# Attention and feed-forward over one core: another order of band and feed-forward work, another choice of PSUM banks, stores issued by ScalarE

## The chip, the core and the metric

One core of a Trainium2 chip runs the whole program, in float32. The metric is the device time of one execution in microseconds. Before the change it is 2633.58 us, the median of three runs (2631.95 to 2634.81).

## What is computed

The input x has the shape (2, 256, 128, 128): batch, time T, band FB, channel C. Three residual blocks follow each other:

```python
xt = _ln(x, ln_t_w, ln_t_b).transpose(0, 2, 1, 3)
x = x + _mha(xt, t_wi, t_bi, t_wo, t_bo, 4, causal_mask).transpose(0, 2, 1, 3)   # over time
xf = _ln(x, ln_f_w, ln_f_b)
x = x + _mha(xf, f_wi, f_bi, f_wo, f_bo, 4, band_mask)     # over bands, |i - j| <= 16
xn = _ln(x, ln_n_w, ln_n_b)
h = gelu(xn @ w1.T + b1)                                   # 128 -> 512
x = x + (h @ w2.T + b2)
```

Each attention has 4 heads of 32 channels.

## The kernel before

The work is cut into 384 groups of 512 tokens (NT = 4 tiles of 128). The first 128 groups (`OverTime`) do attention over time and write to DRAM. Then 16 runs follow, each of 8 groups of attention over bands (`OverBands`) and then 8 feed-forward groups (`FeedForward`) on the same tokens. I call them the first to eighth band group and feed-forward group of a run.

`BoundedPath.run` is one loop over n, a software pipeline written out by hand: step n does the scores or the first hidden products of group n, the weighing of group n - 1, the output of group n - 2, and prepares later groups. Every engine keeps the order in which the instructions are written (`InOrder`), so that order alone decides who runs when, and a waiting instruction holds all behind it on its engine.

A group passes through these stages:

- `load` fetches its tokens with a DMA on SyncE, 14 steps ahead; `statistics` (VectorE) and `root` (GpSimd) make mean and inverse deviation.
- `normalize` makes xh in 4 VectorE instructions; `turn` transposes it in blocks of 32 by 32 into z (VectorE) and writes z to the DRAM tile `turned` in 4 DMAs on SyncE; `fetch` reads `turned` back as xnT, channels on partitions. Step n normalizes and turns group n + 3 and fetches group n + 2.
- Band group: `queries_keys` and `values` multiply xnT by wf on TensorE; `take_query`, `take_key`, `take_values` copy the results from PSUM as qT, kT, v on ScalarE. `first_half` makes the scores, `first_function` limits and masks the fourth head on VectorE and applies exp on ScalarE; `first_mask` masks the other three on GpSimd (tile pf). `weigh` multiplies pf by ones (sums, bank rp) and by v (bank op); `invert` takes ln and exp of the sums on ScalarE, `divide` refines that and scales op to oT on VectorE; `output` multiplies oT by wn, `finish` adds the result to the tokens on VectorE. For the eighth band group of a run `invert_exactly` takes the reciprocal on VectorE, since ScalarE then holds the gelu tables.
- Feed-forward group: `first_half` and `second_half` make two hidden products each (xnT by w1f), `gelus` on ScalarE write hT, `weigh` multiplies hT by w2T into one bank zp (16 products), `divide` adds it to res on VectorE, and `store` writes two groups' results at once with 4 DMAs on SyncE.

A product is 4 matmuls side by side, of 32 weight columns each (`product`); in float32 the profile shows each as two matmul records with a weight load each. PSUM has 8 banks of 512 floats. In band and feed-forward steps `bank` hands them out in turn (`turn_of_bank`), with a few held back (`path.held`, `follow`); in the time steps the banks are named.

In a step of the runs TensorE gets, in this order:

```python
do(n, "first_half", "first_function", "first_mask")
do_at(n + 3, (OverBands, FeedForward), "normalize", "turn")
do(n - 1, "weigh")
do(n - 1, "invert_exactly" if turn else "invert")
do(n - 2, "output", "finish")          # band steps
do(n - 1, "divide")
do(n, "second_half", "second_function")
do_at(n + 1, OverBands, "queries_keys", "take_query", "take_key")
do_at(n + 1, OverBands, "values", "take_values")
```

Of the kernel before, what the change touches and what calls it, by code (L numbers as in the profile page):

```python
# [19 lines left out]
P = 128  # L20
H = 4
# [4 lines left out]
NT = 4  # L26
# [343 lines left out]
class Group:  # L370
# [7 lines left out]
    def __init__(self, path, src, dst, before=None, store=None):  # L378
        self.path, self.src, self.dst = path, src, dst
        self.before, self.store = before, store  # L380

# [76 lines left out]
    def turn(self):  # L458
# [3 lines left out]
        z = path.work.tile([P, H, P], F32, name="z", bufs=2)  # L462
# [98 lines left out]
class Attention(Group):  # L561
    which = None
    swapped = ()
# [7 lines left out]
    def queries_keys(self):  # L571
        path = self.path
        wf = path.k.wf[self.which]
        self.qp = path.bank([P, NT * P], "qp", self.place.get("qp", path.held.pop("qp", None)))
        product(path, self.qp, wf[:, 0:P], self.xnT)

        self.kp = path.bank([P, NT * P], "kp", self.place.get("kp"))
        product(path, self.kp, wf[:, P : 2 * P], self.xnT)

    def take_query(self):  # L580
        path = self.path
        self.qT = path.work.tile([P, NT * P], F32, name="qT")
        path.scalar.activation(self.qT, self.qp, AF.Identity, bias=path.k.bq[self.which], scale=1.0)

    def take_key(self):
        path = self.path
        self.kT = path.work.tile([P, NT * P], F32, name="kT")
        path.scalar.copy(self.kT, self.kp)

    def values(self):  # L590
        path = self.path
        wv = path.k.wf[self.which][:, 2 * P : 3 * P]
        self.vp = path.bank([P, NT, P], "vp", self.place.get("vp"))
# [3 lines left out]
    def take_values(self):  # L597
        path = self.path
        self.v = path.work.tile([P, NT, P], F32, name="v", bufs=4)
        path.scalar.copy(self.v, self.vp)  # L600

# [13 lines left out]
    def divide(self):  # L615

        path, vector = self.path, self.path.vector
        if self.r0 is None:
# [3 lines left out]
            vector.tensor_scalar(self.oT, u, -1.0, None, ALU.mult)  # L622
            return
# [4 lines left out]
        vector.tensor_tensor(by_rows(self.oT), by_tile(self.op), by_tile(u), ALU.mult)  # L628

    def output(self):  # L630
        path = self.path
        self.yp = path.bank([P, NT, P], "yp", self.place.get("yp", path.held.pop("yp", None)))
# [3 lines left out]
    def finish(self):  # L636
        self.path.vector.tensor_tensor(self.dst(), self.yp, self.dst(), ALU.add)
        if self.store is not None:
# [14 lines left out]
class OverTime(Attention):  # L653
# [7 lines left out]
    def values(self):  # L661
        path = self.path
        wv = path.k.wf[self.which][:, 2 * P : 3 * P]
        self.vp = [path.bank([P, 2, P], "vp", self.place.get(f"vp{s}")) for s in range(2)]
# [5 lines left out]
    def take_values(self):  # L670
        path = self.path
        self.v = path.work.tile([P, NT, P], F32, name="v", bufs=4)
        for s in range(2):
            path.scalar.copy(self.v[:, 2 * s : 2 * s + 2], self.vp[s])

    def first_tiles(self):
# [3 lines left out]
        self.s0 = {h: path.bank([P, 2, 2 * P], "sp", path.banks[f"a{h}"]) for h in range(H)}  # L680

    def second_tiles(self):
# [3 lines left out]
        self.s1 = {h: path.bank([P, 2, P], "sp", path.banks[f"b{h}"]) for h in range(H)}  # L686
# [15 lines left out]
    def first_weights(self, heads):  # L702
        for h in heads:
            self.path.scalar.activation(self.p0[:, :, h], self.s0[h], AF.Exp)

    def second_weights(self, heads):
        for h in heads:
            self.path.scalar.activation(self.p1[:, :, h, 0], self.s1[h], AF.Exp)

# [803 lines left out]
```

## Time and profile before

| what | value |
|---|---|
| median of three runs | 2633.58 us |
| profiled execution: span on the page (it gives no other time of it) | 2631.9 us |
| TensorE matmuls busy | 2617.8 us, 99% |
| VectorE, GpSimd, ScalarE busy | 2140.8, 1958.6, 1838.8 us |
| DMA, mean over the span | 131 GB/s |
| chain that ended last | 99% TensorE matmuls |
| granted TensorE clock | 1.000 |

The time groups take the first 934 us of the span, the 16 runs the rest. The end of a matmul is modelled in such a profile, and matmuls overlap, so the busy share of TensorE says little on short delays; the starts of its blocks say more. In the timeline a row gives start, length, engine, operation, tiles written and read, shape and count; in square brackets stands how long the engine was idle before and who ended that. In rows of stretches come the length, then busy time and number of instructions of each engine, the clock, the share of the DMA engines and their rate. In rows of waits come the sum, the number and the longest. DMA rows of the page give the size and the time from issue to landing.

### The profile page before, as it was taken

The numbers are of one execution on the slowest core, as the hardware profiler recorded it, in microseconds if no ns is written. First come the engines' busy times: TensorE is split into PE (matmuls) and PEld (weight loads), VectorE is DVE, ScalarE is ACT, GpSimd is POOL, SyncE is SP. The second block draws the span as 40 slices with busy tenths as digits, with TensorE's granted clock in tenths as the row PEclk, the third lists the DMA queues.
The fourth block names the chain that finished last, engine by engine and source line by source line (L and its number), as shares of the span: only waits on it lengthen the run. The fifth ranks groups of instructions, "written<-read, shape, count | busy, mean of one in ns | idle before, by whom it ended". The sixth has DMA issues, their size and how long they took to land.

```text
span 2631.9 us, 156460 instructions
## 1 busy us (share of the span) xinstructions
PE 2617.8 (99%) x68688; PEld 1837.4 (70%) x68688; DVE 2140.8 (81%) x6410; ACT 1838.8 (70%) x3543; POOL 1958.6 (74%) x2311
## 2 busy tenths in 40 slices
PE   9999999999999999999999999999999999999999
PEld 6666666666766767666777776667676677777776
DVE  8888888888888887977878779788797797887974
ACT  7989988999899875564655746647557466475573
POOL 7999999999999987666667666665776666757762
PEclk9999999999999999999999999999999999999999
DMA  6656555565565454445454544554454445554543
GB/s 155 167 149 158 149 149 149 155 155 149 149 158 149 122 127 119 115 123 127 118 124 124 123 122 117 126 128 120 122 126 120 120 119 131 123 120 123 123 104 88
DMA packets 469797, 344.97 MB, mean 131 GB/s; under 512 B 43120, under 2 KB 404464, under 8 KB 469104
## 3 DMA queue, kind: packets, MB, share of 16 engines
q1 hardware_dynamic: 468408, 334.41, 50.5%
q8 instruction: 540, 8.85, 1.5%
q14 instruction: 153, 1.25, 0.2%
q10 hardware_dynamic: 696, 0.46, 0.1%
HBM read 167.98 MB, written 166.72 MB: 127 GB/s over the span
## 4 chain that ended last, share of the span: by engine, by line
PE 99%; DVE 0%; issue 0%; DMA 0%; ACT 0%; ACTq 0%; DVEq 0%
PE bank L907 99%; DMA x<-in_x 0%; DVE xh L907 0%; DVE bank L907 0%; DVE res L907 0%; DVE stats L907 0%; DVE oT L907 0%; DVE u L907 0%; DVE xnT L907 0%; ACTq L907 0%; ACT p L907 0%; DVE vy L907 0%; ACT lnv L907 0%; DVE mv L907 0%; ACT root L907 0%
## 5 line engine op out<-in xcount | busy, mean ns | idle before, releaser
L907 ACT ACTIVATE hT<-bank,b 128x512 f32<-128x512 f32 x512 | 348.1, 688 | 524.2 <-PE bank L907 483.2
L907 POOL TENSOR_SCALAR_AFFINE_SELECT pf<-pf 128x512 f32<-128x512 f32 x768 | 477.7, 637 | 185.3 <-ACT pf L907 159.1
L907 PEld LDWEIGHTS bank<-w2T_sb,hT 128*32 128x32 f32 x16384 | 467.4, 110 | 54.8 <-issue 29.0
L907 PE MATMUL bank<-xnT,wf 128*32 128x512 f32 x4096 | 492.4, 592 | 0.5 <-DVE xnT L907 0.5
L907 PE MATMUL bank<-xnT,w1f 128*32 128x512 f32 x4096 | 486.3, 592 | 0.2 <-issue 0.2
L907 PE MATMUL bank<-w2T_sb,hT 128*32 128x128 f32 x16384 | 482.8, 273 | 1.0 <-issue 1.0
L907 ACT ACTIVATE p<-bank 128x512 f32<-128x512 f32 (+1 forms) x1024 | 430.6, 494 | 62.9 <-PE bank L907 62.9
L907 DVE TENSOR_SCALAR xh<-x,mv,rstd 128x160 f32<-128x160 f32 (+1 forms) x1012 | 394.3, 432 | 59.7 <-POOL rstd L907 49.4
L907 POOL TENSOR_SCALAR_AFFINE_SELECT p<-p 128x1024 f32<-128x1024 f32 (+2 forms) x384 | 364.5, 949 | 57.5 <-ACT p L907 49.1
L907 PEld LDWEIGHTS bank<-wf,xnT 128*32 128x32 f32 x8192 | 243.3, 110 | 144.1 <-issue 101.6
L907 POOL TENSOR_TENSOR p<-p,p 128x512 f32<-128x512 f32 x256 | 324.6, 1291 | 10.6
L907 DVE BATCH_NORM_STATS2 stats<-x 128x6 f32<-128x128 f32 x1536 | 329.0, 276 | 3.4 <-DMA x<-in_x 3.4
L907 POOL TENSOR_SCALAR rstd<-mv 128x4 f32<-128x4 f32 x251 | 57.8, 230 | 361.7 <-DVE mv L907 360.5
L907 PEld LDWEIGHTS bank<-xnT,w1f 128*32 128x32 f32 x4096 | 183.6, 110 | 171.6 <-issue 109.6
L907 PE MATMUL bank<-qT,kT 32*64 32x80 f32 (+4 forms) x16384 | 302.0, 271 | 0.1
L907 PEld LDWEIGHTS bank<-qT,kT 32*64 32x64 f32 x16384 | 260.0, 131 | 51.2 <-ACT kT L907 50.6
L907 DVE TENSOR_TENSOR res<-bank,res 128x512 f32<-128x512 f32 (+1 forms) x259 | 170.3, 658 | 153.3 <-PE bank L907 144.7
L907 ACT ACTIVATE pf<-bank 128x512 f32<-128x512 f32 x512 | 265.8, 602 | 35.5 <-PE bank L907 31.3
L907 PE MATMUL bank<-wn,oT 128*32 128x128 f32 x8192 | 283.8, 274 | 0.1
L907 DVE STREAM_TRANSPOSE z<-xh 128x512 f32<-128x512 f32 x380 | 270.3, 711 | 13.3
L907 PE MATMUL bank<-wf,xnT 128*32 128x128 f32 x8192 | 276.5, 273 | 0.0
L907 POOL TENSOR_TENSOR rstd<-rstd,mhalf 128x4 f32<-128x4 f32 x251 | 260.8, 1039 | 20.9
(100 smaller groups left out, 3820.3 us busy)
## 6 DMA issues: line engine op xcount, KB each, us to landing
turned<-z SPq DMA_DIRECT2D x1520, 64.0 KB, 2.7
xnT<-turned SPq DMA_DIRECT2D x380, 256.0 KB, 3.2
x<-res SPq DMA_DIRECT2D x256, 128.0 KB, 2.5
x<-x SPq DMA_DIRECT2D x128, 256.0 KB, 4.1
out<-res SPq DMA_DIRECT2D x252, 128.0 KB, 2.3
x<-in_x SPq DMA_DIRECT2D x124, 256.0 KB, 4.3
x<-in_x SPq DMA_DIRECT2D x4, 128.0 KB, 2.8
x<-in_x SPq DMA_DIRECT2D x6, 64.0 KB, 2.9
```

The source lines that it names most:

```text
L907: return self.tc.keep_in_program_order(emit(*args, **kwargs))
```

## The change

Five things change, all in the order of work and the choice of banks.

1. In a step whose group and whose next group are both band groups (`bands[2] and bands[3]`), the queries of group n + 1 come before the weighing of group n - 1, and qT is taken right after the inverse of that group; keys and values stay where they were. TensorE's row in a band step, before and then with the change (wf_238 makes queries, keys and values, pf is the weights after exp, the 64x80 rows are scores):

```order
L907 MATMUL bank_112<-pf,ones 32x512 x4
L907 MATMUL bank_113<-pf,v 32x128 x16
L907 MATMUL bank_110<-wn_241,oT 32x128 x16
L907 MATMUL bank_111<-xnT,wf_238 32x512 x4
L907 MATMUL bank_114<-xnT,wf_238 32x512 x4
L907 MATMUL bank_115<-wf_238,xnT 32x128 x16
L907 MATMUL bank_108<-qT,kT 64x80
```

```order
L967 MATMUL bank_108<-qT,kT 64x80
L967 MATMUL bank_109<-xnT,wf_238 32x512 x4
L967 MATMUL bank_114<-pf,ones 32x512 x4
L967 MATMUL bank_113<-pf,v 32x128 x16
L967 MATMUL bank_110<-wn_241,oT 32x128 x16
L967 MATMUL bank_115<-xnT,wf_238 32x512 x4
L967 MATMUL bank_112<-wf_238,xnT 32x128 x16
```

One of the two 512-wide products with wf moved from behind the output to the place between the scores and the sums.

2. In a step between two feed-forward groups (`weigh_around`) the third hidden product stands between the two halves of the weighing of the group before, the fourth behind it. TensorE, one feed-forward step, before and with the change (w1f makes hidden products, w2T weighs them):

```order
L907 MATMUL bank_109<-xnT,w1f 32x512 x4
L907 MATMUL bank_110<-w2T_sb,hT 32x128 x64
L907 MATMUL bank_111<-xnT,w1f 32x512 x4
L907 MATMUL bank_112<-xnT,w1f 32x512 x4
L907 MATMUL bank_113<-xnT,w1f 32x512 x4
L907 MATMUL bank_114<-xnT,w1f 32x512 x4
```

```order
L967 MATMUL bank_114<-xnT,w1f 32x512 x4
L967 MATMUL bank_115<-w2T_sb,hT 32x128 x32
L967 MATMUL bank_112<-xnT,w1f 32x512 x4
L967 MATMUL bank_115<-w2T_sb,hT 32x128 x32
L967 MATMUL bank_110<-xnT,w1f 32x512 x4
L967 MATMUL bank_108<-xnT,w1f 32x512 x4
L967 MATMUL bank_111<-xnT,w1f 32x512 x4
```

The block of 64 matmuls is cut in two, with one hidden product between.

3. `turn_ahead`: from the second run on, the steps of the last three feed-forward groups also normalize and turn the fourth to sixth band group of the next run, and the first two band steps the seventh and eighth. Band steps three to five then have no normalize. VectorE in the step of the sixth feed-forward group, before and with the change (xh and z are normalize and turn, res is the sum after the weighing):

```order
L907 TENSOR_SCALAR xh<-x,mv,rstd 128x5x32 x4
L907 STREAM_TRANSPOSE z<-xh 128x512
L907 TENSOR_TENSOR res<-bank_108,res 128x512
L907 BN_STATS stats<-x 128x6 x4
L907 BN_AGGR mv<-stats 128x2 x4
```

```order
L967 TENSOR_SCALAR xh<-x,mv,rstd 128x5x32 x4
L967 STREAM_TRANSPOSE z<-xh 128x512
L967 TENSOR_SCALAR xh<-x,mv,rstd 128x5x32 x4
L967 STREAM_TRANSPOSE z<-xh 128x512
L967 TENSOR_TENSOR res<-bank_109,res 128x512
L967 BN_STATS stats<-x 128x6 x4
L967 BN_AGGR mv<-stats 128x2 x4
```

A second normalize and turn stands ahead of res; z has three buffers in place of two, `turned` eight in place of three. On SyncE the transposes' DMAs move with them: 8 in these steps, none in band steps three to five.

4. Stores of feed-forward results are issued two steps later (`put`), on ScalarE while the step's group is a feed-forward group, between the second and third gelu; on SyncE otherwise. The last four groups store as before.

5. PSUM banks are taken from a list of free ones, the one that was released first (`take`, `give`), in place of turns.

The core of the diff:

```diff
+    def take(self, name, shape, i=None):
+        free = self.path.free
+        if i is None:
+            i = free[0]
+        if i in free:
+            free.remove(i)
+        self.taken[name] = i
+        return self.path.bank(shape, name, i)
...
+    def weigh_around(self, other):
+        self.zp = self.take("zp", [P, NT, P])
+        self.weigh_tiles(range(0, 2))
+        other.hidden((2,))
+        self.weigh_tiles(range(2, NT))
+        other.hidden((3,))
...
+    def put(self):
+        if not self.prompt:
+            self.store()
...
+        def turn_ahead(n):
+            for i in (n + 3, n + 6):
+                ahead = at(n + 3, OverBands) and at(i, OverBands) and i not in run0
+                if not at(i, OverTime) and (i == n + 3 or ahead) and not at_turn(i):
+                    do(i, "normalize", "turn")
...
+            self.storing = self.scalar if feeds[2] and n < len(groups) - NT else self.sync
+            do_at(n - 2, FeedForward, "put")
...
-            do_at(n + 3, (OverBands, FeedForward), "normalize", "turn")
+            turn_ahead(n)
...
-            do(n - 1, "weigh")
+            if bands[2] and bands[3]:
+                do(n + 1, "queries")
+            if feeds[1] and feeds[2]:
+                groups[n - 1].weigh_around(groups[n])
+            else:
+                do(n - 1, "weigh")
             do(n - 1, "invert_exactly" if turn else "invert")
+            if bands[2] and bands[3]:
+                do(n + 1, "take_query")
...
-            do_at(n + 1, OverBands, "queries_keys", "take_query", "take_key")
+            if bands[2] and bands[3]:
+                do(n + 1, "keys", "take_key")
+            else:
+                do_at(n + 1, OverBands, "queries_keys", "take_query", "take_key")
```

More of the change, by code (lines that the diff above doesn't have):

```diff
@@ L663, in values @@
         wv = path.k.wf[self.which][:, 2 * P : 3 * P]
-        self.vp = [path.bank([P, 2, P], "vp", self.place.get(f"vp{s}")) for s in range(2)]
+        self.vp = [self.take(f"vp{s}", [P, 2, P], self.place.get(f"vp{s}")) for s in range(2)]
         for i in range(NT):
@@ L815, in weigh @@
         path = self.path
-        path.held = {name: path.turn_of_bank() for name in self.follow}
-        self.rp = path.bank([P, NT * P], "rp")
+        self.rp = self.take("rp", [P, NT * P])
         for h in range(H):
@@ L823, in weigh @@
             )
[L824 removed]
+        self.op = self.take("op", [P, NT * P])
         for i in range(NT):
```

110 lines of the change are left out of this document (76 added, 34 removed).

## The prediction

> **What bounds the kernel now.** I read the page first, then the stretches of the 15 full runs (a run is 8 band groups and 8 feed-forward groups), then the timeline of one run, then who waited. The page says TensorE is the bound, and its queue holds one weight load to each matmul. Queue q8 carries 8.85 MB, 64 bytes for each of those 137,376 instructions: it is TensorE's program.
>
> ```profile
> PE 2617.8 (99%) x68688; PEld 1837.4 (70%) x68688; DVE 2140.8 (81%) x6410; ACT 1838.8 (70%) x3543; POOL 1958.6 (74%) x2311
> q8 instruction: 540, 8.85, 1.5%
> ```
>
> A busy PE is not a PE without delays, so I measured what one step costs undisturbed. Feed-forward: from one w2T block to the next.
>
> ```profile
> 1423.95 3.73 PE L907 MATMUL bank<-w2T_sb,hT 128*32 128x128 f32 x126
> 1427.44 0.60 PE L907 MATMUL bank<-xnT,w1f 128*32 128x512 f32 x2
> 1430.88 3.73 PE L907 MATMUL bank<-w2T_sb,hT 128*32 128x128 f32 x126
> ```
>
> That is 6.93 us: 3.49 of w2T and 3.44 of four hidden products, 0.86 each. A band step:
>
> ```profile
> 1376.24 1.90 PE L907 MATMUL bank<-xnT,wf 128*32 128x512 f32 x16
> 1377.96 1.06 PE L907 MATMUL bank<-wf,xnT 128*32 128x128 f32 x32
> 1378.95 0.97 PE L907 MATMUL bank<-qT,kT 32*64 32x80 f32 x64
> 1379.84 1.06 PE L907 MATMUL bank<-pf,ones 128*32 128x512 f32 x8
> 1380.73 1.06 PE L907 MATMUL bank<-pf,v 128*32 128x128 f32 x32
> 1381.60 1.06 PE L907 MATMUL bank<-wn,oT 128*32 128x128 f32 x32
> 1382.47 0.61 PE L907 MATMUL bank<-xnT,wf 128*32 128x512 f32 x4
> ```
>
> That is 6.23 us: queries and keys 1.72, values 0.99, scores 0.89, sums 0.89, p times v 0.87, output 0.87. A run at this pace takes 8 x 6.23 + 8 x 6.93 = 105.3 us. The 15 full runs took (the first, one of the shortest, the sum):
>
> ```profile
> 933.85:1041.82 107.97, 107.97 (x2790) 1.00 0.50 123
> 1362.03:1467.74 105.71, 105.71 (x2758) 1.00 0.48 120
> sum 1593.21, PE 1590.17; mean PE 106.01
> ```
>
> So 1593.2 - 15 x 105.3 = 13.7 us is all that a better order in the runs can win; some 1.5 of it is one-time work in the first run (2,790 matmuls against 2,758). The granted clock is 1.00 throughout. The time phase (until 933.85) keeps its order.
>
> **What the 13.7 us consist of.** First, stops of TensorE with no semaphore behind them:
>
> ```profile
> PE bank L907 <- issue: 2.7, 7, 0.8
> 1143.75:1175.50 31.75, 31.10 (x896) 21.35 (x896) 25.89 (x61) 24.57 (x45) 20.25 (x33) 1.00 0.48 119
> 1568.60:1599.60 31.00, 30.81 (x896) 19.90 (x896) 25.66 (x60) 24.24 (x45) 19.98 (x34) 1.00 0.46 115
> ```
>
> The two stretches run from one such stop to the next; each holds 896 + 896 = 1792 = 7 x 256 instructions, and 256 x 64 bytes is one q8 packet. So TensorE stops where a block of its program ends and the next has not come. The seven idle times make 2.7; each hides about 0.17 more, since an end is modelled 0.27 after its start and the next starts 0.10 after it: 3.9 us. Stops too short for that list I put at 0.7 (estimate): 4.6. Each also shifts the steps behind it; 1.3 for that (estimate).
>
> Second, the end of each run. In the last feed-forward step ScalarE has two gelus, qT and kT in a row, and the scores wait for kT:
>
> ```profile
> 1349.98 0.69 ACT L907 ACTIVATE hT<-bank,b 128x512 f32<-128x512 f32 x1 [3.66 <-PE bank L907]
> 1350.84 0.69 ACT L907 ACTIVATE hT<-bank,b 128x512 f32<-128x512 f32 x1 [0.17 <-PE bank L907]
> 1351.70 0.69 ACT L907 ACTIVATE qT<-bank,bq 128x512 f32<-128x512 f32 x1 [0.17 <-PE bank L907]
> 1352.56 0.59 ACT L907 COPY kT<-bank 128x512 f32<-128x512 f32 x1 [0.17 <-PE bank L907]
> 1352.16 1.22 PE L907 MATMUL bank<-wf,xnT 128*32 128x128 f32 x32
> 1353.31 0.97 PE L907 MATMUL bank<-qT,kT 32*64 32x80 f32 x64
> ...
> 2517.89 1.23 PE L907 MATMUL bank<-wf,xnT 128*32 128x128 f32 x32
> 2519.04 0.97 PE L907 MATMUL bank<-qT,kT 32*64 32x80 f32 x64
> ```
>
> Values to scores is 1.15 here, 0.99 in the steady step: 0.16, in 6 of 15 runs (first and last shown), and half of it in 2 more: 1.1 us.
>
> Third, VectorE in the later band steps. Its limiting of the fourth head, once a step, comes at
>
> ```profile
> 1380.45 0.67 DVE L907 SCALAR_TENSOR_TENSOR bank<-bank,band 128x512 f32<-128x512 f32 x1
> 1386.98 0.67 DVE L907 SCALAR_TENSOR_TENSOR bank<-bank,band 128x512 f32<-128x512 f32 x1
> 1393.53 0.67 DVE L907 SCALAR_TENSOR_TENSOR bank<-bank,band 128x512 f32<-128x512 f32 x1
> 1394.11 1.60 DVE L907 TENSOR_SCALAR xh<-x,mv,rstd 128x160 f32<-128x160 f32 x4
> 1394.23 0.60 ACT L907 ACTIVATE pf<-bank 128x512 f32<-128x512 f32 x1 [0.15 <-DVE bank L907]
> 1395.74 0.71 DVE L907 STREAM_TRANSPOSE z<-xh 128x512 f32<-128x512 f32 x1
> 1396.73 1.13 PE L907 MATMUL bank<-wf,xnT 128*32 128x128 f32 x32
> 1397.79 0.97 PE L907 MATMUL bank<-qT,kT 32*64 32x80 f32 x64
> ```
>
> every 6.54 us where TensorE needs 6.23: VectorE falls 0.31 behind in each step that has a normalize and statistics, until the exp waits for it, then ln, r, qT, kT, and the scores come 1.06 after the values. Such waits, of 0.07 to 0.8, I sum to 2.0 over the runs. The rest, 13.7 - 1.5 - 4.6 - 1.3 - 1.1 - 2.0 = 3.2, is the output of the eighth band group waiting for its exact reciprocal and small waits.
>
> **The change, part by part.** It adds and removes no arithmetic.
>
> Queries ahead of the weighing (TensorE). A product is 8 matmuls and 8 loads. Densest now: scores (128 instructions), sums (16), p times v (64), 48 of the output: 256 in 0.89 + 0.89 + 0.87 + 0.65 = 3.30 us. With the queries behind the scores: 0.89 + 0.86 + 0.89 + 0.87 + 0.44 = 3.95. Feed-forward: 256 of w2T in 3.49; with a hidden product after each half, 1.75 + 0.86 + 1.53 = 4.13. So a block gets some 0.64 us longer to arrive. Of the seven stops, the longest (0.8 + 0.17) would keep 0.35, the others (0.3 to 0.6 with the 0.17) vanish: 3.9 - 0.35, and 0.5 of the short ones: 4.1. From both sides: nothing, if the transfers are late by something else; 4.6 and the shifts behind them, if all go. I take 4.1 and 1.2 of the shifts, since the stops' own length is the nearest row.
>
> qT then comes off the chain into kT: ScalarE takes it once the queries are done, 2.6 us before the keys. In the run's last feed-forward step the third gelu moves ahead of the second w2T half, so only one gelu, qT and kT follow. Counted from the end of the fourth hidden product, the gelu and qT take 2 x 0.86 = 1.72, which is when the keys end; kT then takes 0.17 + 0.59 and is there at 2.5, and the values end at 1.72 + 0.87 = 2.6. The 1.1 goes.
>
> Normalizing early (VectorE). One normalize is 1.60 + 0.71 = 2.3 us. Fourth to sixth group move to the last three feed-forward steps, so band steps three to five lose 2.3 of their 6.5; the feed-forward steps hold two normalizes, one statistics (0.86 + 0.36) and one res (0.69), 6.5 of 6.93: it fits, with nobody near (the first consumer is a step away). The lag of 0.31 starts only in the last steps: 1.7 of 2.0. The rest term gives perhaps 1.4 of 3.2, through less lag before the reciprocal: between 0 and 3.2, taken below the middle since the reciprocal itself stays.
>
> Stores on ScalarE. SyncE takes 3.0 for four; ScalarE's own issues at the start are 0.46 each, so 1.8 to 3.0.
>
> ```profile
> 0.80 0.92 ACTq L907 DMA_DIRECT2D x<-in_x  x2
> 1423.54 1.49 ACT L907 ACTIVATE hT<-bank,b 128x512 f32<-128x512 f32 x2 [0.23 <-PE bank L907]
> 1428.32 3.02 SPq L907 DMA_DIRECT2D out<-res  x4
> ```
>
> Behind them wait the third and fourth gelu. The second ends 1.08 after w2T starts (1425.03); with stores the third ends by 1.08 + 3.0 + 0.69 = 4.8, and the fourth hidden product ends at 5.2. So nothing is late: cost 0, and SyncE is relieved. What they store was finished a step before. Banks by order of release: in the steady step each is written at least one block after its last reader; 0.
>
> Sum: 4.1 + 1.2 + 1.1 + 1.7 + 1.4 = 9.5. Against the profiled execution's 2631.9 (the page gives its span alone, which equals the lowest run, 2631.95) that is 2622.4; the median shown, 2633.6, is 1.7 above it: 2624.
>
> **Rivals.**
> *The stops stay* (the blocks come late whatever the spacing, or other blocks fall badly): 4.1 and 1.2 are lost, 9.5 - 5.3 = 4.2 remain: 2629. For it: seven stops in some 340 blocks are a tail of the transfer times, and the longest exceeds what is won. Against it: both stops above fall exactly on block ends. The Trainium skill's Runtime: NRT & Kernel Launch, Instruction fetch mechanics, says that the fetch of the next page is mostly hidden, because the sequencer issues more slowly than the pages fill; by that rule this rival would hold with no gain at all from spacing. The trace disagrees with "hidden" here, in seven places and 2.7 us of idle.
>
> *The waits only move*: two normalizes make VectorE late for res or the first band steps, which takes the 1.7, 1.4 and some fetch gain again: 9.5 - 3.1 - 2 = 4.4 at best, worse 0: about 2632. Against it: 6.5 of 6.93.
>
> *The inputs come late* (slower). The queries need xnT 0.89 + 0.87 + 0.87 = 2.6 us earlier. SyncE issues the load only when the transposed pieces have landed:
>
> ```profile
> SPq L907 <- DMA turned<-z: 511.2, 445, 4.3
> 1377.71 0.34 SPq L907 DMA_DIRECT2D xnT<-turned  x1
> xnT<-turned SPq DMA_DIRECT2D x380, 256.0 KB, 3.2
> ```
>
> 1377.71 + 3.2 = 1380.9, used at 1382.47 now: 1.6 spare, 2.6 asked, so 1.0 lost in each of 5 band steps of 15 runs: 75 us less 9.5, about 2699. It decides as soon as the load is not issued 1.0 earlier. Against it: groups four to six are turned three steps sooner, and SyncE's list has no transposes in band steps three to five, so the load follows at once. Only the first run keeps the old place.
>
> **How the numbers follow.** Forecast 0.64, stops stay 0.16, waits move 0.12, inputs late 0.08. A change under 0.2% (5.3 us) can't be told from none. Forecast counts as faster; of stops-stay 0.10 as faster (some spacing gain) and 0.06 as the same; waits-move 0.10 the same, 0.02 slower. Faster 0.74, same 0.16, slower 0.10. Range: below, all 13.7 less the one-time 1.5 and a last run's 0.5, 2633.6 - 12.7 = 2621, and 1.5 for the spread of medians: 2619.5; above, the stops-stay case at 2629 and half a microsecond: 2630. That leaves 0.18 out.
>
> **What would show it.** Right: runs of about 105.5 us each; issue waits on TensorE after 933 of under 1 us; values to scores 0.99 in every step; limiting of the fourth head at a pitch of 6.23 in band steps three to five; four out stores on ScalarE between the second and third gelu. Wrong: TensorE idle on the queries' xnT after the scores, or on res or hT; stops at block ends as before; a feed-forward step over 6.93.

## The result, and the profile after

The changed kernel takes 2647.89 us (median of 5 runs, 2644.80 to 2651.86), the kernel before 2633.58 (5 runs, 2631.95 to 2634.81): a ratio of 1.0052, with a 95% interval of 1.0040 to 1.0064. It is slower by half a per cent, where 2624 was forecast. The profiled execution took 2645.76 us (span 2643.8). Its granted clock is 0.999 against 1.000, and undisturbed steps are as long as before (6.23 and 6.93 us), so the clock does not explain the loss.

The page's busy times, and all waits of TensorE for others in the runs (us in all, times, longest):

```profile
PE 2626.4 (99%) x68688; PEld 1872.6 (71%) x68688; DVE 2143.9 (81%) x6410; ACT 1831.9 (69%) x3543; POOL 1960.4 (74%) x2311
```
```profile
PE bank L967 <- DVE ok L967: 4.2, 1, 4.2
PE bank L967 <- ACT pf L967: 1.5, 1, 1.5
PE bank L967 <- issue: 1.1, 1, 1.1
PE bank L967 <- ACT kT L967: 0.2, 1, 0.2
```

The forecast's mark for the stops ("issue" near 1 us instead of 2.7) is nearly met, and a new wait of 4.2 us, for VectorE's `ok`, stands on top. Both together are far from the 11.9 us by which the span grew. The rest shows only in the lengths of the runs: the first, three others and the sum of the 15 full ones.

```profile
933.46:1048.01 114.55, 110.26 (x2791) 76.52 (x2786) 96.82 (x290) 64.22 (x113) 80.58 (x106) 0.99 0.49 121
1048.01:1154.25 106.24, 106.24 (x2757) 76.95 (x2752) 85.44 (x258) 62.95 (x105) 69.97 (x97) 1.00 0.49 123
...
1687.54:1793.59 106.05, 106.05 (x2757) 76.95 (x2752) 85.47 (x258) 63.05 (x105) 69.93 (x97) 1.00 0.50 125
1793.59:1899.63 106.04, 106.04 (x2757) 76.93 (x2753) 85.45 (x258) 62.93 (x105) 69.95 (x97) 1.00 0.48 119
...
sum 1605.45, PE 1598.24 PEld 1156.72 DVE 1293.21 ACT 946.39 POOL 1059.98; mean PE 106.55 PEld 77.11 DVE 86.21 ACT 63.09 POOL 70.67
```

The sum is 12.2 above the 1593.21 of before: 6.6 in the first run (114.55 against 107.97), 5.7 in the other fourteen. And a run in which nothing special happens takes 106.04, where its best before was 105.70: something costs a little in every run, and TensorE counts as busy all the while.

To find it I cut each run into 16 steps, from the start of one weighing on TensorE to the start of the next, and summed each step over the second to the fifteenth run (worked out from the starts; a start that the moved queries shift by their 0.86 is set back; the step that is left out, from the sums of the eighth group to the first w2T, is 4.32 in both):

| step of the run | before, usual length | after | after less before, 14 runs |
|---|---|---|---|
| band steps 1 to 3 | 5.36, then 6.23 | the same, with single longer ones up to 7.95 | +5.1 |
| band steps 4 and 5 | 6.23, with longer ones up to 7.46 | 6.23 | -4.0 |
| band step 6 (VectorE behind) | 6.23 to 6.49 | 6.21 | -1.5 |
| band step 7 (sums of the eighth group at its end) | 6.06 | 6.48 | +5.6 |
| first feed-forward step (exact reciprocal) | 7.88 to 7.95 | 8.02 | +1.5 |
| feed-forward steps 2 to 6 | 6.93 | 6.93 | -0.4 |
| last full feed-forward step | 8.81 or 8.97 | 8.99 | +1.4 |
| first step of the next run | 7.12, up to 7.85 | 7.12, up to 7.49 | -1.9 |

**The first run.** The rows around the verdict, a product of 6 columns computed once (start, us, engine, what, and in brackets the idle time before it and what ended it):

```profile
1016.24 0.39 PE L967 MATMUL bank<-tests,ones 128*128 128x6 f32 x2
1018.20 0.71 DVE L967 STREAM_TRANSPOSE z<-xh 128x512 f32<-128x512 f32 x1
1018.84 0.65 DVE L967 TENSOR_TENSOR res<-bank,res 128x512 f32<-128x512 f32 x1
1020.46 0.32 DVE L967 TENSOR_SCALAR ok<-bank 128x1 f32<-128x1 f32 x4
1020.84 3.43 PE L967 MATMUL bank<-xnT,w1f 128*32 128x512 f32 x16 [4.21 <-DVE ok L967]
```

`verdict` asks for the bank that is first on the list of free ones, but does not take it off. The hidden product behind it gets the same bank, and has to wait until VectorE, which is busy with normalizing, has read the verdict.

**The step of the masks.** GpSimd's masks and TensorE's sums, before and then after:

```profile
1393.70 0.23 POOL L907 TENSOR_SCALAR rstd<-mv 128x4 f32<-128x4 f32 x1 [1.28 <-DVE mv L907]
1395.02 3.94 POOL L907 TENSOR_SCALAR_AFFINE_SELECT pf<-pf 128x512 f32<-128x512 f32 x6
1398.68 1.38 PE L907 MATMUL bank<-pf,ones 128*32 128x512 f32 x8
```
```profile
1801.80 0.69 DVE L967 TENSOR_TENSOR x<-bank,x 128x512 f32<-128x512 f32 x1 [2.78 <-PE bank L967]
...
1824.69 0.23 POOL L967 TENSOR_SCALAR rstd<-mv 128x4 f32<-128x4 f32 x1 [1.27 <-DVE mv L967]
1825.01 1.04 POOL L967 TENSOR_TENSOR rstd<-rstd,mhalf 128x4 f32<-128x4 f32 x1
1826.02 7.91 POOL L967 TENSOR_SCALAR_AFFINE_SELECT pf<-pf 128x512 f32<-128x512 f32 x12
...
1829.20 1.44 PE L967 MATMUL bank<-pf,ones 128*32 128x512 f32 x6
1830.09 0.61 PE L967 MATMUL bank<-pf,v 128*32 128x128 f32 x8
1830.47 0.60 PE L967 MATMUL bank<-pf,ones 128*32 128x512 f32 x2
```

Before, six masks end at 1395.02 + 3.94 = 1398.96, 0.28 after the sums begin; three of the four heads are masked one after the other, so only the last is late, and barely. After, the first six of the twelve end at 1826.02 + 3.95 = 1829.97, 0.77 after the sums' start. Six of the eight sums start at 1829.20, the two of the head masked last only at 1830.47, and in between TensorE runs p times v for other heads. That is why this wait stands in no list: one group of 32 columns waits, the others go on, and TensorE is "busy". The length of the step shows it. Here the Trainium skill's TensorEngine Tiling (Array Packing), Key Properties, fits: tiles operate independently and can load weights and multiply in parallel. The trace agrees, with those two products 1.27 us behind the other six.

**The last feed-forward step.** Values, kT, scores:

```profile
1782.22 0.69 ACT L967 ACTIVATE hT<-bank,b 128x512 f32<-128x512 f32 x1 [1.40 <-PE bank L967]
1783.08 0.69 ACT L967 ACTIVATE qT<-bank,bq 128x512 f32<-128x512 f32 x1 [0.17 <-PE bank L967]
1783.54 1.22 PE L967 MATMUL bank<-wf,xnT 128*32 128x128 f32 x32
1783.94 0.59 ACT L967 COPY kT<-bank 128x512 f32<-128x512 f32 x1 [0.17 <-PE bank L967]
1784.69 0.97 PE L967 MATMUL bank<-qT,kT 32*64 32x80 f32 x64
```

Values to scores is 1.15, now in nearly every run, though ScalarE waits 1.40 us in front of the last gelu: it is not late. kT starts 0.40 after the values start. The experiments say more on where the 0.16 is from.

### The profile page after: what moved, and what is told of

It reads as the page before. It is cut to its first block, busy times and chain, and to the rows that moved or that the text cites. A ratio compares the mean times of both kernels' runs of the same rounds, so it can differ in the third digit from the quotient of the medians.

```text
span 2643.8 us, 156378 instructions
## 1 busy us (share of the span) xinstructions
PE 2626.4 (99%) x68688; PEld 1872.6 (71%) x68688; DVE 2143.9 (81%) x6410; ACT 1831.9 (69%) x3543; POOL 1960.4 (74%) x2311
## 4 chain that ended last, share of the span: by engine, by line
PE 96%; DVE 2%; POOL 1%; DMA 0%; ACT 0%; issue 0%; ACTq 0%; DVEq 0%; POOLq 0%
PE bank L967 96%; POOL pf L967 0%; DVE xh L967 0%; DVE stats L967 0%; POOL rstd L967 0%; DMA xnT<-turned 0%; ACT pf L967 0%; DVE z L967 0%; DVE mv L967 0%; DVE res L967 0%; DVE ln L967 0%; DMA x<-in_x 0%; POOL x L967 0%; DVE x L967 0%; DVE gs L967 0%
## 5 line engine op out<-in xcount | busy, mean ns | idle before, releaser
L967 PEld LDWEIGHTS bank<-w2T_sb,hT 128*32 128x32 f32 x16384 | 517.1, 110 | 87.8 <-issue 26.9
L967 PE MATMUL bank<-xnT,w1f 128*32 128x512 f32 x4096 | 547.6, 594 | 4.2 <-DVE ok L967 4.2
L967 PE MATMUL bank<-w2T_sb,hT 128*32 128x128 f32 x16384 | 534.1, 273 | 0.0
L967 PE MATMUL bank<-xnT,wf 128*32 128x512 f32 x4096 | 514.7, 595 | 1.2 <-DMA xnT<-turned 0.5
L967 PE MATMUL bank<-wn,oT 128*32 128x128 f32 x8192 | 290.5, 274 | 0.3 <-issue 0.2
L967 PEld LDWEIGHTS bank<-xnT,w1f 128*32 128x32 f32 x4096 | 207.2, 110 | 109.6 <-issue 39.1
L967 DVE TENSOR_TENSOR bank<-bank,r 128x512 f32<-128x512 f32 x240 | 166.9, 695 | 102.2 <-PE bank L967 79.1
```

What stands on the lines that cost most here:

```text
L967: return self.tc.keep_in_program_order(emit(*args, **kwargs))
```

## The experiments

On the chips of the experiments the kernel before took 2630.5 to 2632.4 us (medians); ratios are to its runs beside each, with 95% intervals. By its ratio the changed kernel would take about 2645.5 there. The lengths are worked out as above. A step's length is the commonest one, and the full run is that of runs without a longer step (of e6 the median).

| kernel | us | ratio | step 7 | reciprocal | last | full run |
|---|---|---|---|---|---|---|
| changed | 2647.9 | 1.0052 (1.0040 to 1.0064) | 6.48 | 8.02 | 8.99 | 106.04 |
| e1 bank | 2639.5 | 1.0030 (1.0019 to 1.0041) | 6.46 | 8.02 | 9.00 | 106.04 |
| e2 roots | 2643.8 | 1.0044 (1.0031 to 1.0058) | 6.06 | 8.40 | 8.83 | 105.86 |
| e3 stores on SyncE | 2651.9 | 1.0076 (1.0062 to 1.0090) | 6.46 | 8.02 | 9.00 | 106.04 |
| e4 queries back | 2637.7 | 1.0025 (1.0015 to 1.0034) | 6.06 | 7.88 | 8.81 | 105.35 |
| e5 w2T in one piece | 2644.0 | 1.0050 (1.0037 to 1.0064) | 6.46 | 8.02 | 8.99 | 106.03 |
| e6 no early normalizing | 2652.1 | 1.0074 (1.0060 to 1.0087) | 6.06 to 6.70 | 8.02 | 8.99 | 107.3 |
| e7 all orders undone | 2636.3 | 1.0016 (1.0006 to 1.0025) | 6.06 | 7.88 | 8.82 | 105.72 |
| e8 queries in first step | 2631.4 | 0.9996 (0.9987 to 1.0006) | 6.06 | 7.88 | 8.83 | 105.32 |
| e9 stores behind gelus | 2631.5 | 0.9995 (0.9986 to 1.0004) | 6.06 | 7.88 | 8.83 | 105.33 |
| e10 finish behind divide | 2753.0 | 1.0454 (1.0437 to 1.0470) | 6.06 | 7.81 | 8.83 | 112.65 |
| e13 banks alone | 2630.6 | 1.0001 (0.9992 to 1.0010) | 6.06 | 7.95 | 8.97 | 105.70 |
| e14 output ahead | 2648.7 | 1.0069 (1.0056 to 1.0083) | 6.06 | 7.86 | 8.94 | 106.69 |
| e15 stores of before | 2629.8 | 0.9995 (0.9986 to 1.0004) | 6.06 | 7.88 | 8.83 | 105.32 |

### The verdict's bank (e1)

```
-        tp = self.bank([P, 6], "tp", self.free[0])
+        i = self.free.pop(0)
+        tp = self.bank([P, 6], "tp", i)
...
+        self.release(i)
```

> The changed kernel, with the bank of the verdict's product taken off the list of free banks until VectorE has read it. Theory A (a one-time wait for a bank): in the first run the hidden product right behind the verdict waited 4.46 us for VectorE's ok, and three waits of 0.39 us followed; the step was 13.27 us where the kernel before took 7.54. With a bank of its own it goes back to about 7.5 and the step behind it from 7.18 to 6.93: 2647.9 - 6.0 = 2641.9 us, all other steps as in the changed kernel. Rival (VectorE is simply late there, whatever bank): the step stays above 12 us and the time at 2647.9.

The bank is given back behind VectorE's reads. The step went from 13.27 to 7.54 us, that behind it from 7.18 to 6.93, and the time to 2639.5, 6.0 below the 2645.5. Theory A holds: 6 of the 14 us come from a bank that was not taken off the list.

### The root behind the masks (e2)

```
-            if n + 4 in early:
-                do(n + 4, "root")
...
             do(n, "first_half", "first_function", "first_mask")
+            if n + 4 in early:
+                do(n + 4, "root")
```

> The changed kernel, with GpSimd's root of an early feed-forward group put behind the masks of the step instead of in front of them. Theory B (masks late): queries in front of the sums push the output product 0.86 us back, VectorE's finish, divide and statistics hang on it, the root on the statistics, and the masks stand behind the root; the sums of the last band group but one wait for the masks, 0.41 us in every run (6.48 against 6.06 us). Without the root in front, that step is 6.06 to 6.10 in every run: 16 x 0.4 = 6 us, 2641.8 us. Rival C (ScalarE's exps are late since qT stands in front of them): the masks can't start earlier, the step stays at 6.48 and the time at 2647.9. The last band step's output, which waits for the exact reciprocal, may move by 0.1 either way in both.

Step 7 came back to 6.06 as theory B has it, and the exps were early enough: rival C falls. But the time fell by 1.7 only, not 6, and the intervals of the two overlap. The root, now behind the masks, delays the normalize and with it the exact reciprocal behind that on VectorE, and the output of the eighth group waits for its oT, in 14 runs:

```profile
PE bank L967 <- DVE oT L967: 5.2, 14, 0.4
```

The reciprocal's step grew from 8.02 to 8.40. The lateness was handed on, not taken away.

### Who issues the stores (e3)

```
-            self.storing = self.scalar if feeds[2] and n < len(groups) - NT else self.sync
+            self.storing = self.sync
```

> The changed kernel with all stores of the results issued by SyncE again. Theory D (ScalarE's issues are hidden, as predicted): the last feed-forward step stays at 9.85 us in every run; a store on SyncE's list in front of loads can only make an xnT later: 2647 to 2650 us. Rival E (3.0 us of issues between the second and the third gelu hold qT and kT up): that step goes from 9.85 to 9.69 in all 15 runs, 15 x 0.16 = 2.4 us less: 2645.5 us.

The last step stays at 9.00 (9.86 by its shifted start), so rival E falls. The time is some 6 us above the changed kernel's (the intervals just touch), where theory D allowed 2 (2650 against 2647.9). TensorE's waits for xnT are 1.2 us in the profiled execution, and the first steps of the runs are longer by up to 1.1; the rest of the 6 is not explained.

### Queries back behind the output (e4)

```
-            if bands[2] and bands[3]:
+            ahead = False
+            if ahead:
                 do(n + 1, "queries")
...
-            if bands[2] and bands[3]:
+            if ahead:
                 do(n + 1, "keys", "take_key")
             else:
```

> The changed kernel with the queries of the next band group behind the output again, where they stood before; all other parts kept. Theory B says that the queries ahead cost: the step with the late masks back to 6.06 (-6 us), the step with the exact reciprocal from 8.02 to 7.89 (-2), the xnT late in the second and third band steps gone (-5 in the profiled execution), against some 2 us of stops at the ends of program blocks in the band steps that come back: 2647.9 - 11 = 2637 us. Rival F (the feed-forward order or the two normalizes are what costs): the band steps give nothing and the stops come back: 2648 to 2651 us.

2637.7, as theory B said; rival F falls. All three steps come back at once: 6.06, 7.88 and, in all 15 runs, 8.81. An undisturbed run is 105.35 where the floor of steps is 105.3.

### Feed-forward order, early normalizing (e5, e6)

e5 calls `weigh` and then `second_half` in place of `weigh_around`; e6 has

```
-            for i in (n + 3, n + 6):
+            for i in (n + 3,):
```

> The changed kernel with the second feed-forward product in one piece again (hidden products three and four behind it, as before). On this chip the changed kernel would take about 1.0052 x 2631.8 = 2645.5 us. Theory H (the interleaved feed-forward order does what was predicted, but there is little to do): the stops at block ends in the middle feed-forward steps come back, 1.2 us over the runs of the kernel before and 0.1 with the interleaved order; the last feed-forward step keeps its 0.16, since that comes from columns of TensorE that run apart after the sums waited for masks: 2646 to 2648 us. Rival F (the interleaved order is what costs): the last feed-forward step loses its 0.16 in 15 runs and the one-time wait of 6 us in the first run goes: 2637 us.

> The changed kernel without the early normalizing: groups are normalized and turned three steps ahead, as before; queries still ahead. Theory of the prediction's slower rival (inputs late): the load of xnT stands on SyncE behind transposed pieces that hang on VectorE's normalize of the same step, up to 1.0 us late in each of 5 band steps of 15 runs, 75 us at most: between 2660 and 2720 us, with TensorE idle in front of the queries. Rival (two normalizes in a step cost more than early inputs bring): 2645.5 or less, no idle in front of the queries.

e5 is the same as the changed kernel within the intervals: the interleaved order neither costs nor brings anything that can be measured. Neither theory H's 1 to 2 us nor rival F's gain shows.

e6 is 6 us slower than the changed kernel, and between the two expectations (2660 and more, 2645.5 or less). The waits are there, but they are small:

```profile
PE bank L967 <- DMA xnT<-turned: 16.2, 16, 2.1
PE bank L967 <- DVE ok L967: 2.0, 1, 2.0
```

That is 16.2 us, in 16 of the 75 steps that the expectation counted, where it had up to 75 us. And the wait for the verdict is half as long, since VectorE has one normalize in that step instead of two: half of the 4.2 comes from the early normalizing.

### Banks alone, with later stores and without (e7, e13)

e7 undoes e3, e4, e5 and e6 together and has e1's mending; its stores still come one step later than in the kernel before, on SyncE. e13 adds

```
-        for group in groups[-NT:]:
+        for group in groups:
             group.prompt = True
```

> Banks by order of release alone, with the verdict's bank taken off the list: queries, feed-forward order, normalizing and stores all as in the kernel before. Theory A: the banks cost nothing but the verdict's one wait: 2631.8 us, within 1.5, steps as in the kernel before. Rival G (a bank given last is taken too soon somewhere in the steady steps): above 2636 us, with a step that is longer in every run.

> Banks by order of release alone (the verdict's taken off the list), and now each store right behind its res as in the kernel before; no other part of the change. If the later stores on SyncE made the xnT late (0.25 to 1.13 us in three steps of the variant with the later stores): 2632 us, as the kernel before. If the banks themselves cost: 2636 us again, with a step that is longer in most runs.

e7 takes 2636.3, the rival's number without its sign, since no step is longer in every run; e13 takes 2630.6, as the kernel before. So banks by order of release (with the change's further buffers for z and for what is turned) cost nothing. By the ratios e7 is some 4 us slower than e13, with intervals that overlap a little; the stores are the only difference between them. (The first expectation took the stores for those of before, which they were not.) TensorE's waits in the runs, e7 and then e13:

```profile
PE bank L967 <- issue: 4.9, 9, 1.0
PE bank L967 <- DMA xnT<-turned: 1.2, 2, 1.0
```
```profile
PE bank L967 <- issue: 0.5, 1, 0.5
```

TensorE's order is the same in both. Of the difference only 1.2 us are waits for xnT; the stops at block ends differ by 4.4 us in these two executions, and no run shows whether the later stores cause that.

### Queries ahead in the first band step only (e8), stores behind the gelus (e9), stores of before (e15)

```
-            if bands[2] and bands[3]:
+            ahead = bands[2] and bands[3] and feeds[1]
+            if ahead:
                 do(n + 1, "queries")
```

all three with e1's mending. e9 issues the four stores behind `second_function` where the next step is a feed-forward one; e15 has e13's prompt stores on SyncE.

> The changed kernel with the verdict's bank taken off the list, and the queries ahead only in the first band step of a run, where they stand between the scores and the last w2T product; in the other band steps they are behind the output. Theory: the run with queries behind (2637.7) less the verdict's 6.0, less the stops in that one step (3.1 us over 15 runs with scores right ahead of w2T, 0.7 to 1.5 where queries stood between): 2637.7 - 6.0 - 2 = 2629.7 us, just faster than before (2631.8). Rival (the queries ahead cost in the first band step too, by late xnT): 2632 to 2635 us.

> The version before it (verdict's bank taken off the list, queries ahead only in a run's first band step: 2631.4 us), with ScalarE's four stores put behind the third and fourth gelu of the step where the next step is a feed-forward one. Theory K: a store waits on ScalarE for a res that VectorE, with two normalizes and two statistics in that step, gives late; the gelus behind it come late and w2T waits for them, in the fourth feed-forward step of 6 of 15 runs, 2.85 us in all. Behind the gelus the stores hold nobody up: that step 6.93 in every run, 2628.6 us. Rival (the gelus are late by something else, such as the hidden product): the step keeps its waits, 2631.4.

> Verdict's bank taken off the list, queries ahead only in a run's first band step, early normalizing and interleaved feed-forward order kept, each store right behind its res on SyncE as in the kernel before. Theory (the order of the later band steps is clean at 6.23, the last feed-forward step keeps no 0.16, and no store holds ScalarE up): full runs of 105.33 us but for stops at block ends, 14 x 0.2 to 0.4 us under the kernel before: 2627 to 2629.5 us against 2630.5 to 2632.4. Rival (SyncE's stores make xnT late when two groups are turned in a step): 2632 us or more, with TensorE idle for xnT.

All three end at the kernel before, within 0.1% (2631.4, 2631.5, 2629.8), above the 2628.6 to 2629.7 expected of the first two, and e15 just outside its range. Together with e1, e8 accounts for the whole loss: 6.0 for the bank, 8.1 for the queries in the other band steps. The sign that e15's rival named, TensorE idle for xnT, shows once in its profiled execution, in the first run, which takes 112.21 there (108.52 in e8), though the median doesn't show it:

```profile
1035.31 1.09 PE L967 MATMUL bank<-xnT,wf 128*32 128x512 f32 x8 [2.22 <-DMA xnT<-turned]
```

In e8 theory K's wait is seen on ScalarE, in front of four gelus, with VectorE's res and the stores ahead of it:

```profile
2268.59 0.66 DVE L967 TENSOR_TENSOR res<-bank,res 128x512 f32<-128x512 f32 x1
2269.28 3.57 ACTq L967 DMA_DIRECT2D out<-res  x4
2272.73 0.62 PE L967 MATMUL bank<-w2T_sb,hT 128*32 128x128 f32 x16
2272.89 2.42 ACT L967 ACTIVATE hT<-bank,b 128x512 f32<-128x512 f32 x4 [6.15 <-DMA out<-res]
2273.63 0.43 PE L967 MATMUL bank<-w2T_sb,hT 128*32 128x128 f32 x8 [0.28 <-ACT hT L967]
```

In e9 that step is 6.93 in every run and TensorE waits for no gelu any more, as theory K has it; yet the median doesn't move. What was won (some 2.8 us in one execution) is less than what the stops vary by.

### The cause in the band steps, by two ways round it (e10, e14)

e10 puts VectorE's `finish` behind `divide` and `statistics`; e14 puts the output ahead of the queries, right behind the scores. Both have e1's mending and queries ahead in all band steps.

> The changed kernel with the verdict's bank taken off the list (2639.5 us) and queries ahead in all band steps, but VectorE's finish, which needs the output product, behind divide and statistics, which don't need it. Theory B (VectorE's chain hangs on the output that the queries push back): the step with the late masks goes from 6.46 to 6.06, the one with the exact reciprocal from 8.02 to 7.88, and with the columns together the last feed-forward step from 9.86 to 9.69: 15 x 0.7 = 10 us less, 2629.5 us; somewhat less if stops come back. Rival C (qT on ScalarE in front of the exps is what makes the masks late): these steps stay, 2639.5.

> The changed kernel with the verdict's bank taken off the list (2639.5 us) and queries ahead in all band steps, but the output product ahead of them, right behind the scores; VectorE's order is kept. Theory B (it is the later output): VectorE's finish no longer waits 2.8 us for TensorE, the step with the late masks goes from 6.46 to 6.06, that with the exact reciprocal from 8.02 to 7.88 or less, the last feed-forward step from 9.86 to 9.69: 2639.5 - 10 = 2629.5 us, up to 2632 where the output waits for oT. Rival (queries ahead cost in themselves, by qT in front of the exps): these steps stay as in the changed kernel, 2639.5 or more.

In both the steps that theory B names come back (6.06, 7.81 and 7.86; in e14 the last step only to 8.94), with qT as early as ever: rival C falls again, and it is the later output. But both are slower than e1, by some 112 and 10 us (from the ratios). Waits of TensorE, e10 and then e14:

```profile
PE bank L967 <- DVE x L967: 91.3, 79, 1.6
```
```profile
PE bank L967 <- DVE oT L967: 8.8, 31, 0.7
```

In e10 VectorE begins to read the output's bank 3.95 us after the output starts (1.13 in the changed kernel), and the scores, which take four of the eight banks, wait for it in five steps of each run. In e14 the output would start 0.2 to 0.4 us before VectorE has oT, and four of the band steps are that much longer. I expected 2629.5 of both and had looked at neither who gets the bank next nor when oT is ready.

### The same kernel at other block ends (e11, e12)

```
         self.warm((0, 1, 5, 2))
+        for _ in range(32):
+            self.tensor.matmul(self.bank([P, 6], "tp", 7), self.k.ones, self.k.ident[:, 0:6], start=True, stop=True)
```

in the kernel before; e12 has 64 in place of 32.

> The kernel before with 32 small products of the ones (6 columns, 64 instructions with their weight loads) added at the start, where TensorE warms; nothing else. Theory J (which steps stop depends on where the ends of program blocks fall): all steps of the runs keep their lengths, the stops of 0.2 to 1.0 us (4.9 us in all over the runs of the kernel before) go to other steps, and their sum changes by 1 to 4 us either way; the time moves by that beside what the start takes (at most 5 us, read from when the first sums start). Rival (the dense streams stop wherever the block ends fall): same sum within 1 us.

> The same with 64 small products (128 instructions, half a block). Theory J: a third set of steps that stop, with another sum, 1 to 4 us from the kernel before; what the start takes is read from when the first sums start (at most 10 us). Rival: same sum within 1 us.

The start takes 12.8 and 26.9 us longer (first sums at 39.40 and 53.50 against 26.59), not 5 and 10: 0.4 us for one small product. Less that, the times are 2634.7 and 2632.1 beside 2632.4. Both expectations count half of what was added: each product shows as two matmuls and two weight loads, so 32 products are 128 instructions, half a block, and 64 are 256, a whole block (the page has 68,752 and 68,816 matmuls against 68,688). In e11 the stops moved to other steps, and still sit on block ends: two stretches from one stop to the next hold 1024 = 4 x 256 and 768 = 3 x 256 instructions:

```profile
1050.28:1068.81 18.53, 17.89 (x512) 11.92 (x512) 13.51 (x26) 14.21 (x27) 11.63 (x20) 1.00 0.49 116
1068.81:1082.79 13.98, 13.19 (x384) 9.30 (x384) 13.11 (x37) 10.65 (x20) 9.22 (x15) 1.00 0.47 118
```

e12 has its block ends where the kernel before has them. The longest stop of its runs sits in front of the same product of the second run as one of before (before, then e12), and three of the kernel before's longer first steps of a run (7.85, 7.82, 7.52) are longer again (7.98, 7.43, 7.98); others of its stops are gone:

```profile
1061.86 0.31 PE L907 MATMUL bank<-pf,v 128*32 128x128 f32 x4 [0.41 <-issue]
1087.88 0.31 PE L907 MATMUL bank<-pf,v 128*32 128x128 f32 x4 [1.05 <-issue]
```

The sum (stops of 0.19 us and more at block ends, in the runs of one execution) is 2.9 in e11 and 3.9 in e12, against 4.9 in the kernel before. So theory J is right on the places, by e11. On the sum it is not decided: e12, with the ends where they were, already differs by 1.0.

## Why the prediction was wrong, point by point

The sum had a gain of 9.5 us, and the change costs 14. Two things that the forecast put at nothing made the loss: the banks (0 in the sum; 6.0 measured, e1) and the output and what hangs on it, pushed back by the queries (no term at all; 8.1 measured, e8). And the gains don't show in the time: e8, which is rid of both and keeps the other parts of the change, takes 0.9996 of the kernel before. The base of the sum was right by chance: the span of 2631.9 is not the lowest run's time, since spans lie some 2 us under the time of the same execution (2643.8 for 2645.76 after the change).

**Stops at block ends (4.1 + 1.2 forecast).** The step of this term that failed is "with the queries behind the scores: 3.95". It looked at the 256 instructions that begin with the scores. The queries were taken from in front of the scores, and there it got denser. After the change TensorE runs

```profile
1806.90 1.06 PE L967 MATMUL bank<-wn,oT 128*32 128x128 f32 x32
1807.78 1.04 PE L967 MATMUL bank<-xnT,wf 128*32 128x512 f32 x8
1808.63 1.06 PE L967 MATMUL bank<-wf,xnT 128*32 128x128 f32 x32
1809.62 0.96 PE L967 MATMUL bank<-qT,kT 32*64 32x80 f32 x64
1810.52 1.06 PE L967 MATMUL bank<-xnT,wf 128*32 128x512 f32 x8
```

and 48 instructions of the output, 16 of the keys, 64 of the values and the 128 scores take 0.65 + 0.85 + 0.99 + 0.90 = 3.39, where the densest of before took 3.30. The dense place was turned round the scores, not thinned. The two longest stops of after (1.3 and 1.7 us by the starts of the products; the list of waits puts the second down to ACT pf) sit on block ends in the scores and right behind them. The first:

```profile
1591.90 0.38 PE L967 MATMUL bank<-qT,kT 32*64 32x80 f32 x11 [1.13 <-issue]
```

Band steps 1 to 3 took 5.1 more, most of it in such stops, while steps 4 and 5 lost some 3 us of theirs (estimate from the starts). In the same sense as above the stops sum to 3.4 (before: 4.9), a count that passes over those inside 512-wide products; but e13 with the order of before has 1.2 and e7 6.8. One execution can't show a gain of this size, and the forecast took a sum of one execution for a property of the order. Where a gain mostly held is the first step of a run, with queries between the scores and w2T: -1.9 here, with 3.1 us above its undisturbed length over the runs of e4 and 0.7 in the changed kernel. With the stores on SyncE it was gone (3.0 in e3, 4.1 in e15). The rival "the stops stay" was nearer than the forecast on this term. The Trainium skill's Runtime: NRT & Kernel Launch, Instruction fetch mechanics, calls the crossing of such a boundary mostly hidden. The traces agree for most of the some 340 block ends in the runs and disagree for a few: 11 stops in the kernel before, and 1.2 to 6.8 us in the executions counted here.

**ScalarE's chain at the end of a run (1.1).** The size was near and the cause wrong. In e9 the same place, on the same engines:

```profile
1881.26 0.69 ACT L967 ACTIVATE qT<-bank,bq 128x512 f32<-128x512 f32 x1 [0.17 <-PE bank L967]
1881.87 1.06 PE L967 MATMUL bank<-wf,xnT 128*32 128x128 f32 x32
1882.12 0.58 ACT L967 COPY kT<-bank 128x512 f32<-128x512 f32 x1 [0.17 <-PE bank L967]
1882.85 0.97 PE L967 MATMUL bank<-qT,kT 32*64 32x80 f32 x64
```

ScalarE waits 0.17 for TensorE there as it does after the change; it is no later in one than in the other. But kT starts 0.25 after the values' first product instead of 0.40, and the values take 1.06 instead of 1.22. TensorE's columns run together here and 0.15 apart there. It seems that they come apart where a part of the sums waits for masks: five of the six runs of the kernel before with a last step of 8.97 have a sixth step of 6.38 to 6.41, and no run with such a sixth step has a shorter last one; e4, e8 and e9, without the wait for masks, have 8.81 or 8.83 in nearly every run; so has e2, where TensorE as a whole waits for oT in between. It does not fit everywhere: two runs of the kernel before with still longer sixth steps (6.49, 7.06) have 8.81, and one of e13 with 6.23 has 8.99. That is a reading of lengths that go together; no run changed the columns alone, and it is not shown.

**VectorE in the later band steps (1.7).** Won and lost in the same place. Step 6 gave 1.5, and steps 4 and 5 about 1 beside their stops (estimate), so the lag itself went, as forecast. But the forecast of a pitch of 6.23 in the third to fifth band steps is wrong: in the run shown the limiting of the third to seventh group starts at 1798.32, 1804.47, 1811.75, 1817.98 and 1824.52, pitches of 6.15, 7.28, 6.23 and 6.54. VectorE has time, and spends it waiting 2.78 us for the output (row above), which the queries push back by 0.86. The forecast had asked who waits for the queries' inputs, and who takes qT; it left out what is queued behind the queries on TensorE (sums, p times v, output) and who waits for that. Finish, divide, statistics, root and masks hang on it in a row, and e4 puts the price, with the benefit of the first step still counted against it, at 7.8 us, e8 at 8.1.

**The rest (1.4) and stores (0).** The reciprocal's step got longer, by 0.11 a run (1.5 over 14), by the same chain. That stores cost nothing on ScalarE holds for the changed kernel only by luck: its gelus wait for them longer than forecast,

```profile
ACT hT L967 <- DMA out<-res: 88.5, 25, 5.3
```

5.3 us at most, and in e1, e4 and e8 TensorE in turn waits 0.3 to 1.1 us for such gelus. "It fits" was counted with one statistics in a step; the step shown for e8 has two, and 2 x 2.3 + 2 x 1.2 + 0.7 = 7.7 us of VectorE do not fit in 6.93. Stored as late on SyncE they seem to cost more (e3, e7: some 6 and 4 us, with intervals that touch or overlap).

**Banks (0).** Right for the steady steps (e13: 1.0001), wrong for the one product that is no `Group`'s: 6.0 us. The diff showed `self.free[0]` in `verdict`; I had read the steady steps only.

**The rivals.** None named this. "Inputs late" had the right sign, at 75 us, by xnT; where it was called forth (e6) it was 16.2. "The waits only move" was the right kind at the wrong place and with too small a price.

## What to carry to other kernels

When an instruction moves forward on the bound engine, list what it is moved past, and follow each of those to the engines that wait for it, not only the mover's own inputs; three steps on, a chain that just met its date (masks ending 0.28 us after the sums began) is the one that pays. A free list needs every user to take and give, the one-time ones above all, because a bank that is lent twice may show as nothing but a wait (4.2 us here). And a gain worked out from stops that depend on where blocks of the program end can't be booked from one trace: take several executions, shift the program by half a block as well, and see whether the sum stays.

## What the runs showed of the hardware that was not expected

A wait of one head's products, that is of one group of 32 columns, leaves TensorE "busy", and the columns seem to stay apart for the eight steps that follow, until all wait for kT: 0.16 us at the end of each run (a reading, not shown). The stops at ends of program blocks kept to multiples of 256 instructions in the kernel before, in e11 and in the changed kernel, where TensorE's semaphore instructions, some 13 a run that the timeline leaves out, have to be counted in. But their sum in the runs went from 1.2 to 6.8 us between two kernels with the same order on TensorE, and from 4.9 to 3.9 with the block ends in the same places (e12); what makes one block late and not another stays open. A product of 6 columns, which shows as two full weight loads and two matmuls, takes 0.40 to 0.42 us at the start of the kernel, about half of a product of 512 columns (0.86 for four side by side).
